# Two-pass attention: maxima carried in the second pass's contraction, queries kept per head of a strip, masks joined, big POOL operations in quarters

## The chip, the cores and the metric

The kernel runs on one core of a Trainium2 chip. The time is that of one execution on the device, in microseconds (us). A core has a matrix engine (PE; its weight loads are shown apart as PEld), a vector engine (DVE), an activation engine (ACT), a general engine (POOL) and a queue engine (SP) that issues DMAs. PE writes its products to PSUM, which has eight banks of 128 partitions by 512 floats; DVE and ACT read them from there. Every engine works through its own instructions in order and waits on semaphores for the others.

## The reference, cut to what matters

The network has two layers over x of shape (8, 512, 256): eight batches of 512 tokens with 256 channels. Each layer normalises, applies attention and adds it with a gate, normalises again and applies a feed-forward part. The change touches only the first layer's attention, which has 16 heads of 16 channels that share one key head and one value head:

```python
q = (x @ Wq + bq).reshape(Bx, Tx, HEADS, HD)      # HEADS = 16, HD = 16
k = (x @ Wk + bk)[:, :, None, :]
v = (x @ Wv + bv)[:, :, None, :]
q = _apply_rope(q, sin, cos, HD)
k = _apply_rope(k, sin, cos, HD)
att = jnp.einsum('bthd,bThd->bhtT', q, k) / math.sqrt(HD)
att = jnp.where(causal, -jnp.inf, att)
att = jax.nn.softmax(att, axis=-1)
out = jnp.einsum('bhtT,bThd->bthd', att, v).reshape(Bx, Tx, Cx)
return out @ Wo + bo
```

The softmax over the keys is causal: query t sees keys 0 to t. After this attention come a mixture of experts (each of 16 experts takes the 64 tokens that choose it most strongly), a linear attention and a gated coupling; they are the same before and after.

## The kernel before, in words

**Layout.** A batch is 4 tiles of 128 tokens. The transposed queries `qT` hold 256 rows as two groups g of 128; a group is four strips of 32 rows, and a strip j holds two heads p of 16 rows each. The shared key is written into every strip twice: `kT[:, p, :]` has the keys in the rows of head p and zeros in those of the other head. A product of a 32-row strip of `qT` with the same strip of `kT[:, p]` so gives head (g, j, p). The products of the four strips overlap in PE. All matrices are in float32, and a float product shows as two matrix instructions in the profile, a bf16 one as one.

**Two passes.** The attention is worked out twice. The first pass (`maxima`, line 632 on) computes the scores with the queries along the partitions, adds a causal mask of -1e30 with a bf16 product on the last 128 columns of each block, and DVE reduces each strip to maxima (`tensor_reduce`, lines 661 and 668). The second pass (`heads_of`, line 695 on) computes the transposed scores, keys along the partitions, takes the maxima off, and ACT writes the exponentials (line 740); POOL sets the keys after the query to zero (`affine_select`, line 744), and the products with the values and a column of ones (line 710) give numerators and denominators.

**Rounds.** For each group g there are five rounds, so ten in each pass and batch (`rounds`, line 626). A round fills four PSUM banks, one per strip, with 512 columns: one block of 512, or two of 384 and 128, or two of 256. A round of the first pass is 4 or 8 products of scores (line 646), as many masks as blocks (line 654) and four reductions; a round of the second is 4 or 8 products (line 725), as many bf16 products with `minus` (line 733) and four exponentials.

**How the maxima reach the second pass.** The maxima are float32 and the product with them is bf16, so lines 675 to 691 split each maximum into three bf16 parts (`m3`): cast, subtract, cast, subtract, cast on DVE. PE transposes the parts (line 688), ACT copies them to `mT`, and the products of line 733 (stationary: `minus`, with -1 in the three rows of a head) take them off the scores in PSUM.

**Order.** The order of instructions on all engines is written out by hand. Each batch is a lane, a Python generator: `made_ready` (normalise, project, rotate, transpose to kT and qT), `maxima`, `heads_of`, `finished` (divide, transpose back, project with Wo, add to x, normalise again, logits of the experts). `Steps.run` advances all lanes by one `yield` a step, in order of their rank, and a new batch starts every 15 steps. So in the steady state a step holds a piece of four batches: a piece of `finished`, of `made_ready`, a round of `heads_of` and a round of `maxima`. In `heads_of` a product with the values takes a step of its own after the 4th, 6th and 9th round and after the last; `maxima` issues its ten rounds in ten steps that follow each other. All PSUM tiles come from one pool of eight banks (`net.mm()`), and a tile waits for the last reader of the one that had its bank before.

**Neighbours on the queues.** `made_ready` puts on DVE the statistics (lines 533, 534), the bias of the projection (570), the rotation (586, 594, 600), and on ACT `xh` (547), `hT` (268), the keys (610) and queries (620). `finished` puts on DVE the reciprocals and `o_tok` (781, 783) and the sums with x (811), on PE the transposes (776, 791) and the product with Wo (805), and on POOL the two products with `mod_row` (844). Line 759 adds the bias to x on POOL.

Of the kernel before, what the change touches and what calls it, by code (L numbers as in the profile page):

```python
# [366 lines left out]
class Steps:  # L367


    def __init__(self):  # L370
        self.starters, self.lanes, self.past = [], [], set()
        self.count = 0

    def start(self, lane, rank):

        self.lanes.append([rank, self.count, lane])
        self.count += 1

    def start_every(self, every, batch, rank):
        def starter():  # L380
            for b in range(B):
                self.start(batch(b), rank)
                for _ in range(every):
                    yield

        self.starters.append(starter())

    def rank(self, rank):

        self.now[0] = rank  # L390
# [5 lines left out]
    def run(self):  # L396
        while self.starters or self.lanes:
            self.starters = [s for s in self.starters if next(s, self) is not self]
            for at in sorted(self.lanes, key=lambda at: at[:2]):
                self.now = at  # L400
                if next(at[2], self) is self:
                    self.lanes.remove(at)

# [11 lines left out]
def layer0(net, steps):  # L415
# [83 lines left out]
    parts = strips(4, 3, 3, "parts")  # L499
    minus = wp.tile([P, 4, P], BF16, name="minus")  # L500
    nc.vector.tensor_scalar_mul(minus, parts.unsqueeze(2).to_broadcast([P, 4, P]), -1.0)


    vaug, m3s = [], []
# [5 lines left out]
    for n in range(2):  # L510
        t = wp.tile([P, NT, 4, 32], BF16, name=f"m3_{n}")
        nc.gpsimd.memset(t, 0.0)
        m3s.append(t)
# [41 lines left out]
    def made_ready(b):  # L555
# [45 lines left out]
        yield  # L601

        kT = fp.tile([P, 2, T], F32, name="kT", bufs=3)
# [5 lines left out]
        for p in range(2):  # L609
            nc.scalar.activation(kT[:, p, :], ps, AF.Copy, scale=even_odd[:, p : p + 1])  # L610
        yield
        qT = fp.tile([P, 2, T], F32, name="qT", bufs=3)
        for g in range(2):
            ps = net.mm()
            for i in range(NT):
                nc.tensor.transpose(
                    ps[:, i * P : (i + 1) * P],
                    qd[:, i, 8 * g : 8 * g + 8, :].rearrange("p h e -> p (h e)"), net.ident,
                )
            nc.scalar.copy(qT[:, g, :], ps)  # L620
            yield
# [7 lines left out]
    def rows_of(j):  # L629
        return slice(32 * j, 32 * j + 32)  # L630

    def maxima(b, kT, qT):


        m3 = m3s[b % 2]
# [3 lines left out]
        for g in range(2):  # L639
            for blocks in rounds:  # L640
                strips = [net.mm() for _ in range(4)]
                for n, (p, a, at) in enumerate(blocks):
                    i = tile_of[a]
                    nk = (i + 1) * P
                    for j in range(4):
                        nc.tensor.matmul(  # L646
                            strips[j][:, at : at + nk],
                            qT[rows_of(j), g, i * P : (i + 1) * P], kT[rows_of(j), p, :nk],
                            start=(n == 0), stop=False, skip_group_check=True,
                        )  # L650
                for j in range(4):
                    for p, a, at in blocks:
                        last = at + tile_of[a] * P
                        nc.tensor.matmul(  # L654
                            strips[j][:, last : last + P], net.identb, maskb,
                            start=False, stop=True, skip_group_check=True,
                        )
                p, a, _ = blocks[0]
                for j in range(4):
# [13 lines left out]
        mx = fp.tile([P, NT, 4, 4], F32, name="mx")  # L673
        for i in range(NT):
            nc.vector.tensor_reduce(mx[:, i], pm[:, :, :, blocks_of[i]], AX.X, ALU.max)
        left = mx
        for r in range(3):
            part = m3[:, :, :, r : 12 : 3]
            nc.vector.tensor_copy(part, left)
            if r < 2:  # L680
                rest = fp.tile([P, NT, 4, 4], F32, name=f"rest{r}")
                nc.vector.tensor_tensor(rest, left, part, ALU.subtract)
                left = rest
            yield
        mT = fp.tile([P, T], BF16, name="mT")
        ps = net.mm(BF16)
        for i in range(NT):
            nc.tensor.transpose(
                ps[:, i * P : (i + 1) * P], m3[:, i].rearrange("p j s -> p (j s)"), net.identb
            )  # L690
        nc.scalar.copy(mT, ps)
        yield
        return mT

    def heads_of(b, kT, qT, mT):
# [7 lines left out]
        def values(n):  # L703
# [13 lines left out]
            oT.append(o)  # L717

        for g in range(2):
            for r, blocks in enumerate(rounds):  # L720
                strips = [net.mm() for _ in range(4)]
                for n, (p, a, at) in enumerate(blocks):
                    c = chunk_of[a]
                    for j in range(4):
                        nc.tensor.matmul(  # L725
                            strips[j][:, at : at + T - c * P],
                            kT[rows_of(j), p, c * P : (c + 1) * P], qT[rows_of(j), g, c * P :],
                            start=(n == 0), stop=False, skip_group_check=True,
                        )
                for p, a, at in blocks:  # L730
                    c = chunk_of[a]
                    for j in range(4):
                        nc.tensor.matmul(  # L733
                            strips[j][:, at : at + T - c * P],
                            minus[rows_of(j), 2 * g + p, :], mT[rows_of(j), c * P :],
                            start=False, stop=True, skip_group_check=True,
                        )
                e = ep.tile([P, 4, T], F32, name=f"e{r % 3}", bufs=1 if r == 2 else 2)
                for j in range(4):
                    nc.scalar.activation(e[:, j, :], strips[j], AF.Exp, scale=scale)  # L740
# [9 lines left out]
                if g == 1 and r == 0:  # L750
                    values(1)
                    yield
                if r == 3:
                    values(2 * g)
                    yield
        wg, bg = net.gated_by(pool, wo, bo, ga)
        yield
        values(3)
        nc.gpsimd.tensor_tensor(
            net.x[b], net.x[b], bg.unsqueeze(1).to_broadcast([P, NT, C]), ALU.add  # L760
        )
        yield
        return oT, wg

    def finished(b, oT, wg):
# [77 lines left out]
        for row, how in zip(mod_rows, (ALU.mult, ALU.add)):  # L843
            nc.gpsimd.tensor_tensor(
                xh2, xh2, row.unsqueeze(1).to_broadcast([P, NT, C]), how
            )
# [8 lines left out]
    def batch(b):  # L855
# [4 lines left out]
        mT = yield from maxima(b, kT, qT)  # L860
        past.add(("maxima", b))
        steps.rank(2)
        oT, wg = yield from heads_of(b, kT, qT, mT)
# [992 lines left out]
```

## Time and profile before

| what | value |
|---|---|
| median of three runs | 1194.4 us (1190.34 to 1194.87) |
| the profiled execution | 1192.85 us, its span 1191.1 us |
| mean granted clock of PE | 0.967 |
| first instruction of line 646, last of line 733 | 28.1 us, 499.0 us |
| scores of the first pass, line 646 | 1024 instructions, 136.4 us busy |
| scores of the second pass, line 725 | 1024 instructions, 106.5 us busy |
| products with the split maxima, line 733 | 512 instructions, 43.3 us busy |
| masks of the first pass, line 654 | 512 instructions, 43.1 us busy |
| reductions of the first pass, lines 668 and 661 | 320 instructions, 158.8 and 39.7 us busy |
| exponentials, line 740 | 320 instructions, 164.8 us busy |
| POOL's 128x1024 operations, lines 759 and 844 | 8 and 16 instructions, 2.36 and 2.39 us each |

How to read it: busy time is the time in which at least one instruction of the group ran; instructions of PE overlap, so the busy times of lines add up to more than PE's, and since their ends are modelled, a busy PE is not PE at its peak. In a group's row, the words after the bar give the busy time in us, the mean duration of one instruction in ns, and the idle time of the engine just before the group with the group that ended it. In a timeline, columns are the start, the time covered, the engine, line and operation, output and inputs, and how many; brackets give the idle time before and what ended it.

### The profile page before, as it was taken

Reading aid. Unit: us, or ns where it says so; the run is one execution under the profiler, and the core shown is the slowest. Engines: PE = TensorE matmul, PEld = TensorE weight load, DVE = VectorE, ACT = ScalarE, POOL = GpSimd, SP = SyncE. Lnnn points to the kernel's source line nnn. Section 1 sums busy time; section 2 is a strip of 40 time slices with the busy share of each in tenths; the row PEclk is TensorE's granted clock in tenths of the full one; section 3 lists DMA queues with packets and bytes.
Section 4 is the critical chain, followed back from the end, with each engine's and each line's share of the span. In section 5 each row is a group of like instructions: output and inputs, shape, how many; then the busy total and the mean of one; then the engine's idle time right before and its main releaser. Section 6 shows DMA issues by size and latency. Waiting matters only on the chain. (4 is left out here: it accounts for less than half of the span.)

```text
span 1191.1 us, 22170 instructions
## 1 busy us (share of the span) xinstructions
PE 1104.4 (93%) x8942; PEld 711.6 (60%) x8942; DVE 709.8 (60%) x1463; ACT 554.8 (47%) x1024; POOL 499.0 (42%) x539
## 2 busy tenths in 40 slices
PE   4879999999999999899798898899999988999996
PEld 3545666666666665478677775466666666444433
DVE  4967676766666666732652224666667655556765
ACT  2145656565555546724322334344444424555444
POOL 3023334444343424477777787455556443000000
PEclk9889999999999999999899999899999988999998
DMA  6200000100000011378758854300000000000202
GB/s 214 68 9 2 2 28 25 28 25 28 25 28 25 28 38 28 115 241 246 186 89 214 206 85 59 99 6 6 6 6 6 6 2 1 0 1 1 71 0 72
DMA packets 67975, 69.11 MB, mean 58 GB/s; under 512 B 10216, under 2 KB 64544, under 8 KB 67872
## 3 DMA queue, kind: packets, MB, share of 16 engines
q1 hardware_dynamic: 55024, 49.32, 13.3%
q0 software_dynamic: 12288, 16.79, 8.2%
q8 instruction: 71, 1.16, 0.4%
q10 hardware_dynamic: 560, 1.58, 0.4%
q14 instruction: 32, 0.26, 0.1%
HBM read 46.38 MB, written 21.01 MB: 57 GB/s over the span
## 5 line engine op out<-in xcount | busy, mean ns | idle before, releaser
L740 ACT ACTIVATE e<-mm 128x512 f32<-128x512 f32 x320 | 164.8, 606 | 103.0 <-PE mm L733 99.1
L668 DVE TENSOR_REDUCE pm<-mm 128x4 f32<-128x512 f32 x256 | 158.8, 683 | 84.8 <-PE mm L654 84.5
L744 POOL TENSOR_SCALAR_AFFINE_SELECT e<-e 128x512 f32<-128x512 f32 x128 | 80.3, 645 | 252.2 <-ACT e L740 252.2
L646 PE MATMUL mm<-kT,qT 32*128 32x128 f32 (+3 forms) x1024 | 136.4, 467 | 1.5 <-DVE o_tok L783 1.4
L1134 POOL DMA_INDIRECT xs<-y,slot x64 | 101.8, 1590 | 33.6 <-issue 13.2
L725 PE MATMUL mm<-qT,kT 32*128 32x128 f32 (+3 forms) x1024 | 106.5, 465 | 0.0
L646 PEld LDWEIGHTS mm<-kT,qT 32*128 32x128 f32 x1024 | 75.1, 187 | 44.7 <-DVE pm L668 10.9
L1642 PE MATMUL mm<-g,cn_w 128*128 128x512 f32 x192 | 98.5, 627 | 0.0
L710 PE MATMUL mm<-e,vaug 128*32 128x512 f32 (+3 forms) x1024 | 77.2, 436 | 3.9 <-POOL e L744 2.5
L725 PEld LDWEIGHTS mm<-qT,kT 32*128 32x128 f32 x1024 | 57.1, 184 | 26.7 <-issue 10.6
L1035 POOL DMA_INDIRECT tok<-xg,gidx x64 | 63.5, 992 | 19.1 <-issue 15.7
L1685 DVE SCALAR_TENSOR_TENSOR m<-th,slope,g 128x512 f32<-128x512 f32 x48 | 33.9, 747 | 60.5 <-ACT th L1678 60.5
L1462 POOL TENSOR_SCALAR_AFFINE_SELECT am<-am 128x1024 f32<-128x1024 f32 x32 | 45.6, 1425 | 54.1 <-ACT am L1460 54.1
L1111 PE MATMUL mm<-ew,hid 128*128 128x256 f32 x256 | 63.5, 393 | 1.3 <-ACT hid L1100 1.3
L1098 DVE TENSOR_SCALAR hid<-mm,eb 128x512 f32<-128x512 f32 x32 | 24.0, 750 | 67.6 <-PE mm L1091 67.6
L1100 ACT ACTIVATE hid<-mm,eb 128x512 f32<-128x512 f32 x32 | 22.0, 686 | 89.9 <-PE mm L1091 89.9
L1091 PE MATMUL mm<-tokT,ew 128*128 128x256 f32 x256 | 61.8, 385 | 0.1
L1116 DVE SCALAR_TENSOR_TENSOR y<-mm,eb,gb 128x512 f32<-128x512 f32 x32 | 23.9, 747 | 62.1 <-PE mm L1111 62.0
L1091 PE MATMUL mm<-hid,ew 128*128 128x256 f32 x256 | 60.5, 379 | 0.0
L1290 PE MATMUL mm<-hT,w1qkv 128*128 128x512 f32 x128 | 60.3, 616 | 0.0
L1642 PEld LDWEIGHTS mm<-g,cn_w 128*128 128x128 f32 x192 | 33.5, 195 | 41.3 <-issue 39.6
L1460 ACT COPY am<-mm 128x512 f32<-128x512 f32 x64 | 34.3, 591 | 43.2 <-PE mm L1448 28.7
(245 smaller groups left out, 2209.0 us busy)
## 6 DMA issues: line engine op xcount, KB each, us to landing
ew<-in_L_ffn_w SPq DMA_DIRECT2D x72, 256.0 KB, 5.8
x<-in_L_attn_x SPq DMA_DIRECT2D x8, 512.0 KB, 8.5
xs<-x SPq DMA_DIRECT2D x8, 512.0 KB, 4.7
xg<-xh SPq DMA_DIRECT2D x8, 512.0 KB, 4.1
x<-xs SPq DMA_DIRECT2D x8, 512.0 KB, 9.1
out<-res SPq DMA_DIRECT2D x16, 256.0 KB, 2.2
ga_row<-gate_a SPq DMA_DIRECT2D x16, 128.0 KB, 3.1
mod_row<-rows SPq DMA_DIRECT2D x16, 128.0 KB, 3.8
```

Source lines behind the costliest of these rows:

```text
L646: nc.tensor.matmul(strips[j][:, at : at + nk], qT[rows_of(j), g, i * P : (i + 1) * P], kT[rows_of(j), p, :nk], start=(n == 0), stop=False, ...
L668: nc.vector.tensor_reduce(pm[:, j, 2 * g + p, first : first + 4], strips[j].rearrange("q (a k) -> q a k", k=P), AX.X, ALU.max,)
L710: nc.tensor.matmul(av[32 * j : 32 * j + 32, c * P :], va[:, c, :], e[:, j, at : at + T - c * P], start=(a == 0), stop=(a == 3), skip_group ...
L725: nc.tensor.matmul(strips[j][:, at : at + T - c * P], kT[rows_of(j), p, c * P : (c + 1) * P], qT[rows_of(j), g, c * P :], start=(n == 0), ...
L740: nc.scalar.activation(e[:, j, :], strips[j], AF.Exp, scale=scale)
L744: nc.gpsimd.affine_select(out=own, in_=own, compare_op=ALU.is_ge, fill=0.0, base=0, pattern=[[0, 4], [1, P]], channel_multiplier=-1,)
L1035: self.net.nc.gpsimd.indirect_dma_start(out=tok[:, n, :], out_offset=None, in_=self.net.xg[half], in_offset=bass.IndirectOffsetOnAxis(ap=s ...
L1091: nc.tensor.matmul(ps[:, o * C : (o + 1) * C], w[i][n][:, k, o * P : (o + 1) * P], src[:, k, :], start=(k == 0), stop=(k == 1),)
L1111: nc.tensor.matmul(ps[:, n * C : (n + 1) * C], hid2[i][:, k, n * P : (n + 1) * P], w[i][2][:, k, :], start=(k == 0), stop=(k == 1),)
L1134: nc.gpsimd.indirect_dma_start(out=net.xs[2 * half + n], in_=y[i][:, n, :], in_offset=None, out_offset=bass.IndirectOffsetOnAxis(ap=self.s ...
L1290: nc.tensor.matmul(ps, w[:, k, n * P : (n + 1) * P], hT[:, k, :], start=(k == 0), stop=(k == 1))
L1642: nc.tensor.matmul(ps, w1[:, k, o * P : (o + 1) * P], g[k][bb], start=(k == 0), stop=(k == 1),)
```

## The change

1. *Maxima as a row of the contraction.* The keys of head p now have -1 in the first of the other head's 16 rows (the bias `minus` of the ACT copy). The queries of head p have zeros in the other head's rows, and, between the passes, the maxima of head p in that first row. The same product of 32 rows then gives score minus maximum. The products with `minus`, the three bf16 parts, `m3` and `mT` are gone. The maxima go to a float tile `mx` in eight small reductions, PE transposes them in float32 (8 instead of 4 transposes), and four `scalar_tensor_tensor` on DVE read the transposes from PSUM and add them to the queries.
2. *Queries once per head of a strip.* `qT` becomes two tiles, one per group, each with both heads: four scaled ACT copies for two. Keys have two buffers instead of three.
3. *Joined masks.* A strip with two blocks gets one mask product over both 128-column pieces: 40 instead of 64 a batch.
4. *Order.* `maxima` follows `ORDER`, with a pause (`None`) in the steps in which `heads_of` works on values. It takes 15 steps instead of 14, `heads_of` 15 instead of 14; `made_ready` pauses one step and then writes the keys and the first group's queries in one step. `Steps` learns to place a lane every n-th step and to interleave groups of instructions; no lane uses it.
5. *POOL in quarters.* The 128x1024 operations on x and `xh2` are issued as four of 128x256.

```diff
-    parts = strips(4, 3, 3, "parts")
-    minus = wp.tile([P, 4, P], BF16, name="minus")
-    nc.vector.tensor_scalar_mul(minus, parts.unsqueeze(2).to_broadcast([P, 4, P]), -1.0)
+    minus = strips(2, HD, 1, "minus")
+    nc.vector.tensor_scalar_mul(minus, minus, -1.0)
...
-        kT = fp.tile([P, 2, T], F32, name="kT", bufs=3)
+        kT = fp.tile([P, 2, T], F32, name="kT", bufs=2)
...
-            nc.scalar.activation(kT[:, p, :], ps, AF.Copy, scale=even_odd[:, p : p + 1])
-        yield
-        qT = fp.tile([P, 2, T], F32, name="qT", bufs=3)
+            nc.scalar.activation(
+                kT[:, p, :], ps, AF.Identity, bias=minus[:, 1 - p : 2 - p],
+                scale=even_odd[:, p : p + 1],
+            )
+        qT = []
         for g in range(2):
...
-            nc.scalar.copy(qT[:, g, :], ps)
+            q = fp.tile([P, 2, T], F32, name=f"qT{g}", bufs=2)
+            for p in range(2):
+                nc.scalar.activation(q[:, p, :], ps, AF.Copy, scale=even_odd[:, p : p + 1])
+            qT.append(q)
             yield
...
+    ORDER = (0, 1, 2, 3, None, 4, 5, None, 6, 7, 8, None, 9)
...
+            ends = [at // P + tile_of[a] for _, a, at in blocks]
+            own = slice(ends[0], ends[-1] + 1, max(ends[-1] - ends[0], 1))
+
+            def hide(j):
+                nc.tensor.matmul(
+                    strips[j].rearrange("q (n k) -> q n k", k=P)[:, own], net.identb,
+                    maskb.unsqueeze(1).to_broadcast([P, len(ends), P]),
+                    start=False, stop=True, skip_group_check=True,
+                )
...
+        for q in ORDER:
+            if q is None:
+                yield
+                continue
...
-        mx = fp.tile([P, NT, 4, 4], F32, name="mx")
         for i in range(NT):
-            nc.vector.tensor_reduce(mx[:, i], pm[:, :, :, blocks_of[i]], AX.X, ALU.max)
-        left = mx
-        for r in range(3):
-            part = m3[:, :, :, r : 12 : 3]
-            nc.vector.tensor_copy(part, left)
...
+            for p in range(2):
+                nc.vector.tensor_reduce(
+                    mx[:, i, :, :, 1 - p, 0],
+                    pm[:, :, p:4:2, blocks_of[i]].rearrange("q j g k -> q g j k"), AX.X, ALU.max,
+                )
+        yield
+        for g in range(2):
+            ps = net.mm()
+            for i in range(NT):
+                nc.tensor.transpose(
+                    ps[:, i * P : (i + 1) * P], mx[:, i, g].rearrange("q j p e -> q (j p e)"),
+                    net.ident,
+                )
+            for p in range(2):
+                nc.vector.scalar_tensor_tensor(
+                    qT[g][:, p, :], ps, even_odd[:, 1 - p : 2 - p], qT[g][:, p, :],
+                    ALU.mult, ALU.add,
+                )
+        yield
...
-                for p, a, at in blocks:
-                    c = chunk_of[a]
-                    for j in range(4):
-                        nc.tensor.matmul(
-                            strips[j][:, at : at + T - c * P],
-                            minus[rows_of(j), 2 * g + p, :], mT[rows_of(j), c * P :],
-                            start=False, stop=True, skip_group_check=True,
-                        )
...
+        for q in ORDER:
+            if q is None:
+                yield from values(len(oT))
+                continue
...
-        nc.gpsimd.tensor_tensor(
-            net.x[b], net.x[b], bg.unsqueeze(1).to_broadcast([P, NT, C]), ALU.add
-        )
-        yield
+        for i in range(NT):
+            nc.gpsimd.tensor_tensor(net.x[b][:, i, :], net.x[b][:, i, :], bg, ALU.add)
```

## The prediction

> **What bounds the kernel now.** I read the page's busy table and costliest groups first, then stretches of one batch each, then the timelines of single engines inside such a stretch.
>
> ```profile
> span 1191.1 us, 22170 instructions
> PE 1104.4 (93%) x8942; PEld 711.6 (60%) x8942; DVE 709.8 (60%) x1463; ACT 554.8 (47%) x1024; POOL 499.0 (42%) x539
> L740 ACT ACTIVATE e<-mm 128x512 f32<-128x512 f32 x320 | 164.8, 606 | 103.0 <-PE mm L733 99.1
> L668 DVE TENSOR_REDUCE pm<-mm 128x4 f32<-128x512 f32 x256 | 158.8, 683 | 84.8 <-PE mm L654 84.5
> ```
>
> By these rows PE is the bound and the other engines wait for it. The changed code runs between 20 and 506 us. Stretches from one batch's transposes of the split maxima (L688) to the next's, whose columns are stretch, length, busy PE, PEld, DVE, ACT and POOL, clock, DMA share, GB/s:
>
> ```profile
> 237.47:295.97 58.50, 58.09 (x620) 36.28 (x617) 39.88 (x84) 33.61 (x65) 23.90 (x31) 1.00 0.09 27
> 295.97:354.47 58.50, 58.09 (x620) 36.27 (x617) 39.87 (x84) 33.60 (x65) 23.90 (x31) 1.00 0.09 27
> 413.08:467.03 53.95, 52.94 (x588) 31.39 (x585) 33.12 (x69) 29.00 (x57) 18.39 (x24) 1.00 0.10 29
> 467.03:506.50 39.47, 35.75 (x419) 20.66 (x415) 28.24 (x75) 28.86 (x58) 21.14 (x27) 1.00 0.34 99
> ```
>
> A steady batch takes 58.50 us, and PE seems 99% busy. The same stretches cut to one line say otherwise: in each the first pass's scores (L646) are busy 17.00 us, the second pass's products of equal count and size (L725) 12.90. The excess is waiting inside a group. The timeline shows for what, first of PE, then of DVE:
>
> ```profile
> 250.67 0.39 PE L733 MATMUL mm<-mT,minus 32*128 32x512 bf16 x3
> ...
> 251.97 0.72 PEld L646 LDWEIGHTS mm<-kT,qT 32*128 32x128 f32 x10 [0.33 <-DVE o_tok L783]
> 253.03 0.62 PE L654 MATMUL mm<-maskb,identb 128*128 128x128 bf16 x8
> 253.49 0.39 PE L791 MATMUL mm<-ident,o_tok 128*128 128x128 f32 x2
> 253.81 2.36 PE L710 MATMUL mm<-e,vaug 128*32 128x512 f32 x32
> 256.10 1.14 PE L646 MATMUL mm<-kT,qT 32*128 32x512 f32 x8
> 257.17 0.40 PE L654 MATMUL mm<-maskb,identb 128*128 128x128 bf16 x4
> ```
>
> ```profile
> 248.81 2.48 DVE L668 TENSOR_REDUCE pm<-mm 128x4 f32<-128x512 f32 x4 [0.84 <-PE mm L654]
> 251.50 0.42 DVE L783 TENSOR_TENSOR o_tok<-mm,att_r 128x256 f32<-128x256 f32 x1
> 253.36 2.48 DVE L661 TENSOR_REDUCE pm<-mm 128x4 f32<-128x512 f32 x4 [1.44 <-PE mm L654]
> 257.44 2.48 DVE L668 TENSOR_REDUCE pm<-mm 128x4 f32<-128x512 f32 x4 [1.60 <-PE mm L654]
> 283.55 2.48 DVE L668 TENSOR_REDUCE pm<-mm 128x4 f32<-128x512 f32 x4 [1.38 <-PE mm L654]
> 287.47 2.48 DVE L668 TENSOR_REDUCE pm<-mm 128x4 f32<-128x512 f32 x4
> ```
>
> Four reductions (2.48 us) free four of eight PSUM banks. The last strip of the next round's scores needs one of them, or one freed by a DVE operation queued behind them. It starts 0.05 later; its masks follow at +1.06 (251.97 to 253.03), the next reduction at +0.33. So neighbouring first-pass rounds stand at least 2.48+0.05+1.06+0.33=3.92 us apart (283.55 to 287.47 is 3.92), and 4.59 with a reciprocal and an o_tok (together 0.67) between (248.81 to 253.36 is 4.55). PE sets the pace only where it has more than that to do between two rounds.
>
> **The change, part by part, per batch.** M0 to M9 are the rounds of the first pass, H0 to H9 those of the second.
>
> *The products with the split maxima (L733) go*: 64 in ten rounds, each taking 0.21 to 0.33 us from start to the next group's start: 2.1 to 3.3, I take 2.7. It shortens PE alone and gives nothing in a round that DVE bounds.
>
> *Joined masks*: 40 instead of 64, with the same columns. Eight of 128 columns take 0.46 (253.03 to 253.49), 57 ns each. Four of 256 are not in the trace: their bounds are 0.23 (as four of 128) and 0.46. I take 0.44, because columns set the spacing of bf16 products here: L733's last 0.39 each at 512 columns, 0.21 at 128. The Trainium skill, "TensorE: Matmul & The Clock Gate", section "Back-to-back issue gap", states about 81 ns per product for a stream of loads and matmuls at 128 columns and 131 at 512; by that each joined round would save about a quarter of a microsecond. The trace's 57 ns disagrees with the 81; the saving is a rival below.
>
> *Maxima*: three casts, two subtractions (0.23 each) and an ACT copy (0.67) go. Added: eight small reductions for four (0.13 apart, 1.0), eight float transposes (0.11 apart as L776, 0.88) for four bf16 ones (0.33), four scalar_tensor_tensor of 128x512 from PSUM. L1116 is that operation, 747 ns; groups of L668 issue 0.06 closer than their 683 ns, so 0.69 each, 2.8; bounds 2.5 (L668's 0.62) and 3.5 (L1300's 874 ns). They queue on DVE ahead of the next batch's M0, and H0 waits for the queries that they rewrite, where before only L733 waited for the maxima.
>
> *Queries once per head of a strip*: four scaled copies for two, +1.3 on ACT (0.65 as L610), which is busy 33.6 of 58.5. Between H9's exponentials and M0 it does two hT (0.66 apart), six copies (0.55) and an oT: done 7.0 after H9, while PE needs their banks at 7.7. Values(3), 2.29 on PE, hides it; without that up to 1.6 would show.
>
> *POOL in quarters*: three operations of 2.36 become twelve, by 0 to 3x0.20 longer in sum (0.20 as L541, 128x4). POOL is busy 23.9; the softmax masks (L744) queued behind wait up to 1.8 more, and values need them only rounds later. Zero.
>
> *Two key buffers for three*: by the order of instructions the keys of batch b+2 are written after H9 of batch b; zero, up to 1 if ACT stood there. SP's queue keeps its order: its DMAs move along.
>
> *Pauses*: M now rests where H stops for a value product, and every M has an H beside it. Before, three of the products (2.29) stood between two M rounds and covered reductions. So I add up the distances between first reductions anew, in the changed order, with starts from above and from the same stretch: H or M 0.97, L805 1.78, four L566 products 2.09, L263 0.53, L791 0.31, strip-to-reduction 1.44 (the loop's 0.05+1.06+0.33):
>
> - M9 to M0: masks 0.11, five groups of transposes 2.5, values(3) 2.29, first transposes of maxima 0.64, scalar_tensor_tensor 2.8: 8.4. DVE's other 4.6 lies under it.
> - M0 to M1: 2.48, bn 1.1, two reciprocals and o_tok 1.34, 1.44: 6.4.
> - M1 to M2: 4.6. M2 to M3: 4.0.
> - M3 to M4: PE, 2x0.31, 2.29, 0.53, 0.97, bank of hT 0.2, 1.39: 6.0.
> - M4 to M5: PE, 0.11, 1.78, 0.53, 0.97, 0.97, 0.33: 4.7.
> - M5 to M6: PE, 1.78, 2.09, 2.29, 2.09, 0.97, 0.97, 0.33, less 0.1: 10.4.
> - M6 to M7: DVE, 2.48, bn 1.1, rope's 1.44: 5.0.
> - M7 to M8: third reduction 1.86, 1.44: 3.3.
> - M8 to M9: PE, 2.29, 0.97, 0.97, 0.33, less 0.1: 4.5.
>
> That is 57.3 against 58.5: 1.2 gained of the 2.2 that PE loses in work (2.7+0.33+0.1-0.88); the rest becomes longer waits in the rounds that DVE bounds.
>
> **The sum.** Five steady batches 6.0; the first and the last joint batch, the same each, 2.4; H of the last batch alone (39.47 us) 1.5 of its L733 rounds; against it 1.0 for the first batch's scalar_tensor_tensor ahead of any H. That is 8.9. The stages behind are unchanged and move along. The profiled execution took 1192.85 (its span 1191.1 and 1.75 around it), 1.5 below the median of 1194.4: 1184. With the bounds above (masks 0.23, scalar_tensor_tensor 2.5 to 3.5, L733 2.1 to 3.3) and half a microsecond a batch of waits not seen, its own range is 1174 to 1191.
>
> **Rivals.**
> - *The value products cover nothing any more* (0.22, slower). DVE idles in the four pauses while the joint rounds keep the distances of before: M2-M3 4.55, M3-M4 7.2 (4.08, 2.29 and 0.84), M6-M7 5.65, M7-M8 3.92, M8-M9 6.2 (3.92 and 2.29) make the batch 62.0: +3.5 in seven batches, less 0.5: 1217. It decides from 58.5 a batch upward. For it: DVE already waits 13.5 us a batch for masks. Against it: five of the ten distances are sums of PE's work.
> - *The products were hidden anyway* (0.20). PE waits longer for banks by all that it saves, as L646's 17.00 against 12.90 hints; the batch stays at 58.5, the time at 1193. Against it: around L805, L566 and L710 PE runs group after group at its shortest.
> - *A joined mask costs what one of 128 does* (0.06): 0.21 in 6 rounds of 8 batches, 10 us more: 1174. Against it: 57 ns. The Trainium skill's rule named above would give about as much.
> - My forecast has 0.52.
>
> A measurement here tells 0.5% (6 us) from no change. Faster: the last two but a part of 0.05. Same: the hidden products and that part. Slower: the first rival. The range goes down to the third rival and its share of my own bounds, 1171, and up into the first, 1204.
>
> **What would show it.** Some 57 us between two batches' transposes of maxima; exponentials that wait for scores only; four scalar_tensor_tensor within 3 us; M1 waiting for o_tok; masks 0.11 apart; DVE idle in the pauses. I am wrong if a batch exceeds 58.5, if H0 waits over 1 us for its queries, or if masks take half.

## The result, and the profile after

The changed kernel takes 1184.88 us (median of 4 executions, 1180.21 to 1186.25), the kernel before 1194.63 beside it: a ratio of 0.9917, 95% interval 0.9891 to 0.9944. The profiled execution took 1180.21 us, its span 1178.5. The page's busy table and costliest groups answer the rows shown of before:

```profile
span 1178.5 us, 20955 instructions
PE 1093.8 (93%) x8270; PEld 699.6 (59%) x8270; DVE 726.6 (62%) x1487; ACT 562.0 (48%) x1032; POOL 512.7 (44%) x610
L796 ACT ACTIVATE e<-mm 128x512 f32<-128x512 f32 x320 | 164.7, 604 | 80.0 <-PE mm L773 79.3
L716 DVE TENSOR_REDUCE pm<-mm 128x4 f32<-128x512 f32 x256 | 158.6, 681 | 68.0 <-PE mm L683 67.8
```

PE is busy 10.6 us less, the exponentials (L796) wait 80 instead of 103 us for scores, the reductions (L716) 68 instead of 85. The same stretches as before, now from transposes of maxima (L731) to the next, with the same columns; the last ends with the last value product:

```profile
232.95:291.05 58.10, 57.41 (x536) 35.25 (x533) 42.11 (x89) 34.45 (x67) 26.01 (x40) 1.00 0.09 27
291.05:349.16 58.11, 57.40 (x536) 35.24 (x532) 42.11 (x89) 34.46 (x67) 26.02 (x40) 1.00 0.09 27
407.27:457.06 49.79, 49.03 (x500) 29.14 (x497) 35.25 (x73) 29.33 (x57) 19.53 (x32) 1.00 0.11 31
457.06:494.00 36.94, 33.64 (x342) 19.21 (x346) 29.75 (x80) 27.11 (x55) 19.78 (x33) 1.00 0.33 99
```

A steady batch fell from 58.50 to 58.10 only; the last joint stretch, the last in which both passes run, fell from 53.95 to 49.79. With the first transposes of each stretch and the end of the last value product read from both traces (before 68.60, 121.10, 413.08, 467.03 and 503.67; after 67.36, 116.80, 407.27, 457.06 and 493.92), the first attention divides so:

| stretch | before | after | gained | predicted |
|---|---|---|---|---|
| start to the first transposes of maxima | 68.60 | 67.36 | 1.24 | 0 |
| first joint stretch | 52.50 | 49.44 | 3.06 | 0.2 |
| five steady batches | 291.98 | 290.47 | 1.51 | 6.0 |
| last joint stretch | 53.95 | 49.79 | 4.16 | 1.2 |
| second pass alone | 36.64 | 36.86 | -0.22 | 1.5 |
| sum | 503.67 | 493.92 | 9.75 | 8.9 |

The prediction's 1.0 for the first batch's scalar_tensor_tensor stands in the second row (1.2 less 1.0), since they follow that batch's transposes. The first row lies between 67.3 and 69.2 in all traces of kernels with the new order, so its 1.24 is not laid to the change. The stages behind took 687.4 us before and 684.6 after; another execution of the changed kernel has 690.7 there, so this difference isn't laid to it either.

A part of the second row goes with the clock. These are the two first joint stretches, before and after, with the columns from above; the last but two is the granted clock:

```profile
68.60:121.10 52.50, 51.18 (x554) 30.46 (x552) 35.05 (x66) 29.09 (x55) 16.20 (x24) 0.97 0.01 2
67.36:116.80 49.44, 49.22 (x469) 28.39 (x469) 36.78 (x73) 29.49 (x56) 15.75 (x24) 1.00 0.01 2
```

In the traces of kd_later and sind_wo below, which have the changed order and a clock of 0.97 in this stretch, it took 50.11 and 50.06 instead of 49.44. So some 0.6 of the 3.06 is the clock's, an estimate from these three stretches.

The timelines of DVE and of POOL in one steady batch show the seam and the place where the steady batch lost most of what was forecast:

```profile
275.61 0.18 DVE L550 BATCH_NORM_AGGREGATE bn_mv<-bn_st 128x2 f32<-128x6 f32 x1
276.24 1.26 DVE L602 TENSOR_TENSOR cosd<-qkv,rope 128x1088 f32<-128x1088 f32 x1
277.41 2.48 DVE L709 TENSOR_REDUCE pm<-mm 128x4 f32<-128x512 f32 x4
281.83 0.69 DVE L610 TENSOR_TENSOR kd<-cosd,sind 128x512 f32<-128x512 f32 x1 [1.94 <-POOL sind L594]
282.44 2.47 DVE L716 TENSOR_REDUCE pm<-mm 128x4 f32<-128x512 f32 x4
...
288.76 1.07 DVE L298 TENSOR_TENSOR wo_g<-wo,ga_row 128x512 f32<-128x512 f32 x1
289.75 0.95 DVE L300 TENSOR_TENSOR bo_g<-bo,ga_row 128x256 f32<-128x256 f32 x1
290.62 0.75 DVE L723 TENSOR_REDUCE mx<-pm 128x8 f32<-128x8 f32 x8
291.86 2.72 DVE L736 SCALAR_TENSOR_TENSOR qT<-mm,even_odd,qT 128x512 f32<-128x512 f32 x4 [0.49 <-PE mm L731]
```

```profile
276.41 1.14 POOL L554 TENSOR_SCALAR bn_rstd<-bn_mv 128x4 f32<-128x4 f32 x1 [1.26 <-DVE bn_mv L550]
277.63 1.02 POOL L555 TENSOR_TENSOR bn_rstd<-bn_rstd,neghalf 128x4 f32<-128x4 f32 x1
...
279.17 2.63 POOL L594 TENSOR_TENSOR sind<-qkv,rope 128x544 f32<-128x544 f32 x2
281.72 0.26 POOL L606 COPY vaug<-qkv 128x64 f32<-128x64 f32 x1
281.90 2.29 POOL L800 TENSOR_SCALAR_AFFINE_SELECT e<-e 128x512 f32<-128x512 f32 x3
288.55 3.43 POOL L893 TENSOR_TENSOR xh<-xh,mod_row 128x256 f32<-128x256 f32 x4
```

Between M7 (277.41) and M8 (282.44) DVE stands still for 1.94 us. It is at kd, and kd needs sind, which POOL begins only at 279.17, behind the normalisation's chain of four small operations. M8's scores are ready, but its reductions are queued behind kd. The second thing to see is wo_g: 1.07 us here, 0.69 in the kernel before; POOL's quarters of L893 run beside it. DVE and POOL before, where kd stood behind M9's reductions (287.47) and found sind ready:

```profile
289.87 0.68 DVE L594 TENSOR_TENSOR kd<-cosd,sind 128x512 f32<-128x512 f32 x1
...
292.97 0.69 DVE L296 TENSOR_TENSOR wo_g<-wo,ga_row 128x512 f32<-128x512 f32 x1
```

```profile
281.55 0.19 POOL L538 TENSOR_SCALAR bn_rstd<-bn_mv 128x4 f32<-128x4 f32 x1 [2.33 <-DVE bn_mv L534]
```

The first operation of the chain, bn_rstd, takes 1.14 after and 0.19 before. So 0.95 of kd's 1.94 may come from there; this is an estimate, and no run tests it by itself.

### The profile page after: what moved, and what is told of

The parts are those of the page before. It is cut to its first block, busy times and chain, and to the rows that moved or that the text cites. A ratio compares the mean times of both kernels' runs of the same rounds, so it can differ in the third digit from the quotient of the medians.

```text
span 1178.5 us, 20955 instructions
## 1 busy us (share of the span) xinstructions
PE 1093.8 (93%) x8270; PEld 699.6 (59%) x8270; DVE 726.6 (62%) x1487; ACT 562.0 (48%) x1032; POOL 512.7 (44%) x610
## 5 line engine op out<-in xcount | busy, mean ns | idle before, releaser
L796 ACT ACTIVATE e<-mm 128x512 f32<-128x512 f32 x320 | 164.7, 604 | 80.0 <-PE mm L773 79.3
L716 DVE TENSOR_REDUCE pm<-mm 128x4 f32<-128x512 f32 x256 | 158.6, 681 | 68.0 <-PE mm L683 67.8
L673 PE MATMUL mm<-kT,qT 32*128 32x128 f32 (+3 forms) x1024 | 139.3, 462 | 2.4 <-DVE pm L709 0.8
L773 PE MATMUL mm<-qT,kT 32*128 32x128 f32 (+3 forms) x1024 | 113.5, 463 | 0.0
L673 PEld LDWEIGHTS mm<-kT,qT 32*128 32x128 f32 x1024 | 77.8, 189 | 44.6 <-DVE pm L709 12.8
L773 PEld LDWEIGHTS mm<-qT,kT 32*128 32x128 f32 x1024 | 60.2, 183 | 32.6 <-issue 10.9
```

The costliest lines, as they stand in the source:

```text
L673: nc.tensor.matmul(strips[j][:, at : at + nk], qT[g][rows_of(j), p, i * P : (i + 1) * P], kT[rows_of(j), p, :nk], start=(n == 0), stop=Fal ...
L716: nc.vector.tensor_reduce(pm[:, j, 2 * g + p, first : first + 4], strips[j].rearrange("q (a k) -> q a k", k=P), AX.X, ALU.max,)
L773: nc.tensor.matmul(strips[j][:, at : at + T - c * P], kT[rows_of(j), p, c * P : (c + 1) * P], qT[g][rows_of(j), p, c * P :], start=(n == 0 ...
```

## The experiments

Every edit is against the changed kernel unless it says otherwise. "Batch" is the distance between two transposes of maxima in the steady batches. No kernel leaves out work. Distances between first reductions in a steady batch, us (of no_pause one of five batches that differ: 61.3 to 63.1, with M9-M0 from 12.1 to 17.2):

| kernel | M9-M0 | M0-M1 | M1-M2 | M2-M3 | M3-M4 | M4-M5 | M5-M6 | M6-M7 | M7-M8 | M8-M9 | batch |
|---|---|---|---|---|---|---|---|---|---|---|---|
| before | 13.77 | 6.08 | 4.54 | 4.08 | 3.92 | 4.86 | 5.97 | 5.71 | 5.64 | 3.92 | 58.50 |
| predicted | 8.4 | 6.4 | 4.6 | 4.0 | 6.0 | 4.7 | 10.4 | 5.0 | 3.3 | 4.5 | 57.3 |
| after | 8.15 | 6.27 | 4.64 | 4.41 | 5.90 | 4.65 | 10.48 | 4.65 | 5.03 | 3.92 | 58.10 |
| kd_later | 8.16 | 6.27 | 4.64 | 4.41 | 5.90 | 4.65 | 10.48 | 4.65 | 3.25 | 4.79 | 57.21 |
| sind_first | 8.27 | 6.27 | 4.64 | 4.41 | 5.90 | 4.65 | 10.48 | 4.68 | 3.25 | 4.66 | 57.22 |
| zero_products | 8.14 | 6.83 | 4.73 | 4.48 | 5.92 | 4.80 | 10.75 | 4.66 | 5.02 | 3.92 | 59.25 |
| pool_whole | 9.25 | 6.27 | 4.64 | 4.41 | 5.90 | 4.65 | 10.48 | 4.65 | 5.03 | 3.91 | 59.19 |
| whole_wo_early | 7.55 | 6.27 | 4.64 | 4.41 | 5.90 | 4.65 | 10.48 | 4.65 | 5.03 | 4.46 | 58.05 |
| no_pause | 16.24 | 6.28 | 4.64 | 4.41 | 3.98 | 3.86 | 4.61 | 7.58 | 5.64 | 4.65 | 61.89 |

The first four below ran beside a median of 1193.23 us for before, the next four beside 1193.26, the last three beside 1192.97. My theory after the first look was: the ledger of distances is right but for the wait at kd; the gain comes from the products with the split maxima; the joined masks are worth nothing; POOL's quarters were costed wrongly. The rivals were those of the prediction.

**The changed kernel again**, as the ground for what follows.

> The changed kernel once more, as the mark for the experiments beside it: 1185 us, 0.992 of the kernel before, and a steady batch of 58.1 us between two batches' transposes of maxima.

1185.12 us (1184.0 to 1186.64), ratio 0.9929 (0.9912 to 0.9947), batch 58.10, last value product at 494.22.

**kd behind the idle step instead of ahead of it.** In made_ready, the step that the change put behind qd goes ahead of kd:

```diff
         nc.gpsimd.tensor_copy(va[:, :, 0:HD], qkv[:, :, C + HD :])
         yield
+        yield
 
         kd = rp.tile([P, NT, 8, HD], F32, name="kd")
...
-        yield
         yield
```

> The changed kernel with one edit: the idle step of made_ready stands ahead of kd and not behind qd, so that kd falls into the pause of the first pass. Theory (the 5.03 us from M7 to M8 are DVE waiting 1.94 us in kd for POOL's sind, with M8's reductions queued behind): M7 to M8 falls to 3.3 to 3.9, a steady batch to 56.4 to 57.0, the time by 6 to 11 us, 1174 to 1179. Rival (the wait only covers another one, the turn of the banks): M7 to M8 stays above 4.5, the batch above 57.8, the time within 3 us of 1185.

M7-M8 is 3.25 and the batch 57.21: the ledger of the prediction, with its 57.3. The time is 1182.71 (1181.74 to 1184.8), ratio 0.991 (0.9893 to 0.9927). The wait went as the theory has it, but the batch lies 0.2 above the expected range, and the time, 2.4 below after_again, is what the rival named. Five batches by 0.9 are 4.5; the last value product ends only 1.9 us earlier than in after_again (492.28), because the stretch of the second pass alone is 1.3 longer, the first joint stretch 0.7 and the start 0.6. In all three the granted clock of this trace is below that of after_again: 0.96 instead of 1.00, 0.97 instead of 1.00 and 0.82 instead of 0.85. That fits, but no run separates the clock from the edit there.

**No pauses in the first pass.** The change's M rounds rest where H stops for a value product; here they follow each other at once:

```diff
-        for q in ORDER:
+        for q in (*range(10), None, None, None):
```

> The changed kernel with the ten rounds of the first pass in ten steps that follow each other and three idle steps behind them, so that value products stand between first-pass rounds again. Theory (what the pauses lose beside the values they win at the next batch's seam): distances M3 to M4 4.0, M6 to M7 7.5, M9 to M0 12.6, together 58.0 a batch, the time within 4 us of 1185. Rival (value products that cover reductions were worth their 2.29 us each): a batch of 56 or less, 1172 or less.

1212.24 us, ratio 1.0157 (1.0138 to 1.0176), 27 above the changed kernel, and the expectation is missed. The timelines of DVE, POOL and PE of this kernel at the end of a batch:

```profile
230.70 2.48 DVE L716 TENSOR_REDUCE pm<-mm 128x4 f32<-128x512 f32 x4
235.11 0.69 DVE L610 TENSOR_TENSOR kd<-cosd,sind 128x512 f32<-128x512 f32 x1 [1.93 <-POOL sind L594]
...
246.94 2.48 DVE L716 TENSOR_REDUCE pm<-mm 128x4 f32<-128x512 f32 x4 [0.47 <-PE mm L683]
```

```profile
232.46 2.61 POOL L594 TENSOR_TENSOR sind<-qkv,rope 128x544 f32<-128x544 f32 x2
235.01 0.24 POOL L606 COPY vaug<-qkv 128x64 f32<-128x64 f32 x1
235.20 3.70 POOL L800 TENSOR_SCALAR_AFFINE_SELECT e<-e 128x512 f32<-128x512 f32 x3
```

```profile
231.53 1.93 PE L757 MATMUL mm<-e,vaug 128*32 128x512 f32 x24 [0.20 <-DVE pm L716]
236.35 0.64 PE L757 MATMUL mm<-e,vaug 128*32 128x256 f32 x8 [2.89 <-POOL e L800]
```

M9's reductions start at 230.70 and M0's at 246.94. Between them now lie two value products, H9 and all the transposes, while M3 to M6 stand at DVE's pace (3.98, 3.86, 4.61). Besides, PE waits 2.89 us inside the third value product for softmax masks that stand behind sind in POOL's queue. Which of the two makes the 27 us was open; no_pause_sind below takes the second away.

**POOL's operations whole again.**

```diff
-        for i in range(NT):
-            nc.gpsimd.tensor_tensor(net.x[b][:, i, :], net.x[b][:, i, :], bg, ALU.add)
+        nc.gpsimd.tensor_tensor(
+            net.x[b], net.x[b], bg.unsqueeze(1).to_broadcast([P, NT, C]), ALU.add
+        )
...
-            for i in range(NT):
-                nc.gpsimd.tensor_tensor(xh2[:, i, :], xh2[:, i, :], row, how)
+            nc.gpsimd.tensor_tensor(
+                xh2, xh2, row.unsqueeze(1).to_broadcast([P, NT, C]), how
+            )
```

> The changed kernel with POOL's operations on x and xh2 whole again, 128x1024. Theory (quarters only change who waits for whom between POOL and DVE, off the path): wo_g and bo_g go back from 1.08 and 0.95 us to 0.7 and 0.4, the first transposes of the maxima no longer wait some 0.2, the batch is 57.9, the time 1183 to 1185. Rival (quarters shorten the path, as softmax masks and DVE slip between them): a batch above 58.6, the time above 1188.

1190.1 us (1187.77 to 1193.66), ratio 0.9973 (0.9958 to 0.9987). The expectation is missed and the rival's numbers hold: the quarters are worth 5 of the changed kernel's 8 to 10 us. Of the distances only M9-M0 grew, by 1.1. Its timelines of DVE, POOL and PE say why:

```profile
291.62 2.71 DVE L298 TENSOR_TENSOR wo_g<-wo,ga_row 128x512 f32<-128x512 f32 x1
294.25 0.41 DVE L300 TENSOR_TENSOR bo_g<-bo,ga_row 128x256 f32<-128x256 f32 x1
294.58 0.74 DVE L723 TENSOR_REDUCE mx<-pm 128x8 f32<-128x8 f32 x8
```

```profile
291.40 2.37 POOL L893 TENSOR_TENSOR xh<-xh,mod_row 128x1024 f32<-128x1024 f32 x1
```

```profile
294.96 1.18 PE L731 MATMUL mm<-ident,mx 128*128 128x128 f32 x8 [0.98 <-DVE mx L723]
```

wo_g starts 0.22 after L893 and lasts 2.71 instead of 0.69. L893 ends at 293.77; from there to wo_g's end (294.33) is 0.56, about wo_g's own time. I read this as standing still while POOL's instruction ran. The maxima behind it in DVE's queue come late: PE waits 0.98 for them. The Trainium skill, "SBUF — State Buffer", section "Who interferes with whom", says that a VectorE instruction with two SBUF inputs contends with a GpSimd instruction that reads SBUF, and that whoever starts first holds the shared pair of ports for its whole instruction. The trace agrees: both inputs of wo_g are in SBUF, and in quarters it costs 1.07, waiting for one quarter instead of a whole operation. The four reductions from PSUM that run beside POOL's softmax masks in the changed kernel (282.44 and 281.90 above) keep their 2.47.

**Masks one by one.** The joined masks are put back to one product per diagonal block:

```diff
-                nc.tensor.matmul(
-                    strips[j].rearrange("q (n k) -> q n k", k=P)[:, own], net.identb,
-                    maskb.unsqueeze(1).to_broadcast([P, len(ends), P]),
+                for end in ends:
+                    nc.tensor.matmul(
+                        strips[j][:, end * P : (end + 1) * P], net.identb, maskb,
...
```

> The changed kernel with one mask product for each block again, 64 a batch for 40. Theory (columns set the time of masks, 57 ns each at 128): four of 256 and eight of 128 both take about 0.45, no distance moves by more than 0.1, a batch stays within 0.3 of 58.1, the time within 2 us of 1185. Rival (each product costs the same): 0.2 more in the rounds that PE sets, a batch of 58.9 or more, 1190 or more.

1184.22 us (1183.03 to 1186.53), ratio 0.9924 (0.9905 to 0.9944), batch 58.20: 0.1 a batch, nothing that the time shows.

**The products are put back as products of zeros**, 64 in a batch, bf16, of the same shapes and at the places of the old ones:

```diff
+    none = wp.tile([P, P + T], BF16, name="none")
+    nc.gpsimd.memset(none, 0.0)
...
-                    start=(n == 0), stop=True, skip_group_check=True,
+                    start=(n == 0), stop=False, skip_group_check=True,
...
+            def nothing(j, p, a, at):
+                c = chunk_of[a]
+                nc.tensor.matmul(
+                    strips[j][:, at : at + T - c * P],
+                    none[rows_of(j), :P], none[rows_of(j), P + c * P :],
+                    start=False, stop=True, skip_group_check=True,
+                )
...
+            ] + [
+                [functools.partial(nothing, j, *block) for j in js] for block in blocks
```

> The changed kernel with the 64 bf16 products a batch put back in their places, now with zeros, so that PE does the removed work and nothing else differs. Theory (only rounds that PE sets get longer): M3 to M4, M4 to M5, M5 to M6 and M8 to M9 by 0.2 to 0.3 each, M2 to M3 by as much through the exponentials, the rest by under 0.1: a batch of 59.1 to 59.6, the last batch's H 1.5 to 3 more, the time 1193 to 1197. Rival one (hidden anyway): a batch within 0.3 of 58.1, 1188 or less. Rival two (all of PE's work counts): 2.7 a batch, 60.8, 1205 or more.

1197.79 us (1195.49 to 1200.85), ratio 1.0038 (1.0024 to 1.0051); batch 59.25 as expected, time just above it. So the products' removal is worth 12.7 us of time in the new order (13.4 to 13.7 at the last value product, 507.65), more than the whole change gains; without it the rest of the change would lose 0.2 to 0.5%. A steady batch shows 1.15 of it, the first joint stretch 4.1 (53.58 against 49.44), the last 2.7, the second pass alone 0.5. The first joint stretch shows 1.4 more than the last: in this trace the granted clock there is 0.97 instead of 1.00, with 0.50 from 111.0 to 114.4, and the distance M8-M9 in which that lies is 6.58, where the last joint stretch has 4.89. So some 1.4 of the 13.4 is rather the clock's, an estimate.

**POOL's chain of the normalisation one step later** (of both normalisations of a batch), so that sind is issued ahead of it:

```diff
+        yield
         rstd = net.small.tile([P, NT], F32, name="bn_rstd")
...
         yield
-        yield
```

> The changed kernel with POOL's four small operations behind the statistics one step later, so that sind no longer stands behind them in POOL's queue. Theory (kd waits for sind, and sind for that queue): DVE no longer waits before kd, M7 to M8 3.3 to 3.9, M8 to M9 at most 4.6 with no wait of the values for POOL, a batch of 56.9 to 57.3, 1180 to 1183. Rival (the later small operations hold up xh, hT and so the next transposes): M9 to M0 grows by what M7 to M8 loses, the batch stays above 57.8.

1177.43 us (1175.45 to 1178.66), ratio 0.9858 (0.9837 to 0.9879): faster than both kernels and below the expected range. Timelines of POOL and DVE:

```profile
274.24 3.66 POOL L594 TENSOR_TENSOR sind<-qkv,rope 128x544 f32<-128x544 f32 x2
...
279.34 0.51 POOL L555 TENSOR_SCALAR bn_rstd<-bn_mv 128x4 f32<-128x4 f32 x1
```

```profile
279.03 0.77 DVE L610 TENSOR_TENSOR kd<-cosd,sind 128x512 f32<-128x512 f32 x1
279.89 2.48 DVE L716 TENSOR_REDUCE pm<-mm 128x4 f32<-128x512 f32 x4
```

sind starts 2.4 ahead of M7's reductions (276.64) instead of 1.8 behind them, kd waits for nothing, and M8 follows 3.25 behind M7. The batch is 57.22, the last value product ends at 490.66, 3.6 earlier than in after_again; that much of the 7.7 us of time is shown. The rest lies behind that point. Two executions of one kernel differ by as much there, but all five of this kernel lie below all of after_again, so chance alone isn't a likely cause, and it stays open.

**The same, with wo_g and bo_g made in the pause of the third value product:**

```diff
+                if len(oT) == 2:
+                    wg, bg = net.gated_by(pool, wo, bo, ga)
...
-        wg, bg = net.gated_by(pool, wo, bo, ga)
```

> As sind_first, and wo_g and bo_g are made in the pause of the third value product, where DVE idles, and not ahead of the small reductions. Theory: those reductions end about 2 us earlier, the transposes of maxima no longer wait some 0.2 for them, M9 to M0 is 7.9 to 8.0, a batch 0.2 to 0.3 shorter than in sind_first, 1178 to 1182. Rival (wo_g now contends with POOL's sind or softmax masks there and holds the next reductions): M8 to M9 grows by 0.3 or more and the gain is lost.

1176.86 us (1175.4 to 1178.0), ratio 0.9854 (0.9833 to 0.9875); M9-M0 stays at 8.27, batch 57.20. A miss: with quarters, wo_g at its old place isn't what M0 waits for. The two kernels can't be told apart.

**POOL's quarters alone, in the kernel before.**

> The kernel before, with POOL's three large additions and products of a batch in quarters and nothing else of the change. In the kernel before, DVE makes wo_g in 0.69 us at a moment when POOL stands idle (POOL's addition L759 starts 295.04, wo_g ends 293.66), so if whole POOL operations cost time only through wo_g beside them, the quarters bring nothing here: a steady batch of 58.3 to 58.7 us, and 1191.5 to 1195 us beside 1193 for before. Rival: the quarters are a gain of their own wherever they stand, about the 5 us that they are worth in the changed kernel: batch near 57.5, 1188 us.

1195.73 us (1194.66 to 1197.73), ratio 1.0028 (1.0017 to 1.0039), just above the expected range; all distances as before to 0.02, batch 58.50. In the old order the quarters gain nothing.

**Whole POOL operations, and wo_g early** (the edits of pool_whole and of sind_wo's second part):

> The changed kernel with POOL's operations whole again, as in pool_whole, and wo_g and bo_g made during the third value product, where no large POOL operation stands. If the whole operations cost only through wo_g (2.71 us beside L893 instead of 1.07), the distance from M9 to M0 falls from 9.25 back to 8.2 or less, the batch from 59.19 to 58.1, and the time from 1190.1 to 1185. Rival: the whole operations delay something else at the seam too (masks of the exponentials queued behind them, other DVE work beside them): the batch stays above 58.8 and the time above 1188.

1182.48 us (1181.95 to 1184.66), ratio 0.9919 (0.9905 to 0.9932); M9-M0 7.55, batch 58.05. DVE's timeline:

```profile
287.20 0.68 DVE L298 TENSOR_TENSOR wo_g<-wo,ga_row 128x512 f32<-128x512 f32 x1
...
288.13 2.47 DVE L716 TENSOR_REDUCE pm<-mm 128x4 f32<-128x512 f32 x4
```

The whole operations cost only through wo_g: with wo_g at 0.68 beside no large POOL operation they cost nothing, and the quarters aren't needed. M8-M9 grows by 0.5, since wo_g and bo_g now stand ahead of M9's reductions, and M9-M0 falls by about as much against the changed kernel.

**No pauses, with sind_first's edit.**

> The first pass without its pauses, as in no_pause, and POOL's chain of the normalisation one step later, so that sind starts earlier and the softmax masks behind it too, as in sind_first. If the 27 us that the pauses were worth came through POOL's queue (the third value product waits 2.89 us for masks that stand behind sind), the third value product takes under 3 us instead of 5.39, the distance from M9 to M0 falls from 16.24 to about 13.3, the batch to about 59, the time to 1187 to 1193. Rival: the rounds of the first pass bunch up behind DVE and leave both value products and M0's start uncovered whatever POOL does: M9 to M0 stays above 15, the batch above 61, the time above 1203.

1204.59 us, ratio 1.0104 (1.0089 to 1.012). PE's timeline, and ACT's:

```profile
230.51 2.36 PE L757 MATMUL mm<-e,vaug 128*32 128x512 f32 x32 [0.29 <-POOL e L800]
232.80 1.15 PE L773 MATMUL mm<-qT,kT 32*128 32x384 f32 x16
234.63 0.33 PE L265 MATMUL mm<-ident,xh 128*128 128x128 f32 x1 [0.69 <-ACT xh L563]
```

```profile
233.98 1.09 ACT L563 ACTIVATE xh<-x,bn_off,bn_rstd 128x256 f32<-128x256 f32 x2 [1.62 <-POOL bn_off L559]
```

The third value product takes 2.36, but four of the five steady batches stay between 61.7 and 62.4, and M9-M0 between 15.1 and 16.2 in all but the first. Those four have a granted clock of 0.97; the fifth, at 1.00, takes 60.33, where the batches of no_pause at 1.00 take 61.3 to 61.9. So at a clock of 1.00 the edit takes 1.0 to 1.6 us off a batch here, and 0.9 off one with pauses. The times agree: with sind_first's edit on both sides the pauses are worth 27.2 us (1204.59 against 1177.43), without it 27.1. So it isn't POOL's queue that makes them worth 27 us; that the bunching of the M rounds does is argued from the distances. One wait was exchanged for another, too: the chain behind sind now makes xh late, and PE waits 1.65 us for it in four places (0.69, 0.16, 0.64 and 0.16).

## Why the prediction was right, and where it wasn't

The time came out at 1184.9 against 1184.0, faster, as forecast. The cause forecast, less work for PE, holds: zero_products gives it 12.7 us. But the sum behind the 8.9 has errors of both signs: +5.8 in the joint stretches, -4.5 in the steady batches, -1.7 in the second pass alone and +1.2 at the start. That they cancel is luck.

- *Steady batches: 6.0 forecast, 1.5 measured.* The step that failed is "M7 to M8: third reduction 1.86, 1.44: 3.3". It took 5.03. The step has no term for kd, which the new order puts ahead of M8's reductions in DVE's queue, where it waits for POOL's sind. kd_later and sind_first take that wait away in two ways, and both give 3.25 and a batch of 57.2, the forecast's 57.3. M8-M9 (4.5 forecast, 3.92) was the same error with the other sign: M9's scores had their time during kd's wait. This makes 0.8 a batch; the other 0.5 comes from the first of the five, which took 57.87 before and not 58.50.
- *The other distances* hold to 0.4: 8.15 for 8.4, 5.90 for 6.0, 10.48 for 10.4, M6-M7 4.65 for 5.0, 4.41 for 4.0.
- *First and last joint stretch: 1.4 forecast (2.4 less 1.0), 7.2 measured.* The step "the first and the last joint batch, the same each, 2.4" failed. In the joint stretches M9-M0 fell about as far as in a steady batch (at the first's end 13.30 to 7.23, steady 13.77 to 8.15). What M0 to M9 took longer in exchange was 3.2 in the first (39.03 to 42.19) and 1.6 in the last (40.31 to 41.95), against 5.2 in a steady batch (44.72 to 49.95). In the first, M0-M1 falls by 1.40, where it grows by 0.19 in a steady batch, and M7-M8, where kd finds sind ready (3.25), falls by 1.40 instead of 0.61. In the last, which has no kd, M5-M6 grows by 0.86 instead of 4.51. About 0.6 of the first's gain is the clock's, as said above. The 1.0 for the first batch's scalar_tensor_tensor can't be told apart in that stretch.
- *Second pass alone: 1.5 forecast, -0.2 measured.* Up to its third value product the changed kernel gains 1.4: that product starts 27.33 us into the stretch before and 25.96 after. Then it waits 2.40 us for softmax masks, 0.75 before. They stand in POOL's queue behind the normalisation's chain, as sind does in a steady batch, and the chain starts 27.51 into the stretch before and 27.80 after. So what PE gains is lost in this wait. In sind_first the wait is gone, and the stretch takes 37.05 all the same, with 1.94 of waiting for an operation of DVE (L1013) and a granted clock of 0.95 instead of 1.00; so the wait is not the only thing that holds it. PE's timeline and POOL's, before:

```profile
494.36 1.93 PE L710 MATMUL mm<-e,vaug 128*32 128x512 f32 x24
497.03 0.64 PE L710 MATMUL mm<-e,vaug 128*32 128x256 f32 x8 [0.75 <-POOL e L744]
```

```profile
494.54 0.19 POOL L538 TENSOR_SCALAR bn_rstd<-bn_mv 128x4 f32<-128x4 f32 x1 [0.15 <-DVE bn_mv L534]
```

and of the changed kernel:

```profile
483.02 1.93 PE L757 MATMUL mm<-e,vaug 128*32 128x512 f32 x24
487.35 0.64 PE L757 MATMUL mm<-e,vaug 128*32 128x256 f32 x8 [2.40 <-POOL e L800]
```

```profile
484.86 0.20 POOL L554 TENSOR_SCALAR bn_rstd<-bn_mv 128x4 f32<-128x4 f32 x1 [1.59 <-DVE bn_mv L550]
```

- *POOL's quarters: zero forecast, 5 us measured.* The step "POOL in quarters ... Zero" priced only POOL's own time. In the old order zero is right (before_quarters). In the new order wo_g lies beside L893, and whole operations would have held it for 2 us; that cost of the new order was nowhere in my sum, and the quarters, which I priced at nothing, paid for it.
- *Joined masks: right.* Four of 256 columns take 0.45 (start to start, 257.30 to 257.75) as eight of 128 did. The rival with half that is gone: masks_single shows 0.1 a batch. By the 81 and 131 ns that the Trainium skill, "TensorE: Matmul & The Clock Gate", section "Back-to-back issue gap", states for a stream of loads and matmuls, joining would have saved an estimated quarter of a microsecond a round; masks_single shows no such saving.
- *Maxima: right.* Four scalar_tensor_tensor 2.72 (2.8 forecast); the eight small reductions 0.75 instead of 1.0; eight transposes 1.07 to the next group, 0.88 forecast.
- *Queries on ACT, two key buffers: nothing visible*, as forecast; the scalar_tensor_tensor wait for PE's transposes alone (0.49). H0 takes 1.75 to the next group's start (294.54 to 296.29) instead of 0.97. The 0.78 is no wait for its queries, which the first of the four scalar_tensor_tensor had written: the weights of H0's last strip are loaded 0.05 after M0's first reduction (294.50, 0.68 long), which frees a bank. PEld's row:

```profile
295.23 0.29 PEld L773 LDWEIGHTS mm<-qT,kT 32*128 32x128 f32 x2 [0.30 <-DVE pm L716]
```

- *Rival, value products cover nothing:* gone; M3-M4 took 5.90, M6-M7 4.65 and M8-M9 3.92 against its 7.2, 5.65 and 6.2, and the pauses are worth 27 us. Without them a batch takes the 61.3 to 63.1 that the rival wanted (62.0) with them.
- *Rival, products hidden anyway:* its batch (58.5) was nearer to the measured 58.10 than mine. zero_products shows that it is wrong all the same: the products cost 1.15 in a steady batch and 12.7 us in all. They were not hidden; in the steady batches a new wait of 1.9 hid most of their going.

## What to carry to other kernels

Before an operation is counted as hidden under its engine's idle time, look at what it needs and at what is queued behind it: here one DVE operation that waited for POOL held the reductions which free the banks. When an order is changed, look anew at which two-input VectorE operations come to lie beside long GpSimd operations; moving the one, or cutting the other into pieces, both repaired it. And a forecast that fits in the sum should be held against the stretches one by one: here four misses cancelled.

## What was not expected of the hardware

- A DVE operation of 0.68 us took 2.71 beside one GpSimd operation of 2.37 that had started 0.22 earlier, and 1.07 beside the same work in quarters; bo_g's 0.42 became 0.95 in quarters.
- It goes the other way too: POOL's bn_rstd, 0.19 us in the trace of before, took 1.14 when it started 0.17 after DVE's cosd, which reads two SBUF operands for 1.26. In sind_first, where it started 0.31 after kd (279.03, 0.77 long), it took 0.51 and ended 0.05 after kd. I read this as the same contention.
- The stages behind the first attention, which no edit here touches, took 684.6 and 690.7 us in two executions of the same kernel (mean granted clock 0.97 and 0.96 there), so that a gain of 3 us in one stage is better read from the distances in the trace than from the time.
